# The written order behind the last attention: router, far bounds, expert rounds and scatter in a four-layer image kernel

## The chip, the cores and the metric

One core of one Trainium2 chip runs the whole program. The metric is the device time of one execution in microseconds (us); lower is better. The core has five engines that work at the same time and meet through semaphores: TensorE (PE: matrix products and transposes), VectorE (DVE), ScalarE (ACT), GpSimd (POOL) and SyncE (SP, which here only starts transfers). Each engine works through its own list of instructions in the order written. Transfers run on sixteen DMA engines that all queues share.

## The reference

Four images of 56 x 56 points with 128 channels go through four layers. Layer 0 is attention over 7 x 7 neighbours with a multilayer perceptron; layer 1 a gated recurrence in the Fourier domain; neither is touched. Layers 2 and 3 see an image as 3136 tokens:

```python
t = t + L2_attn(ln(t))     # full softmax attention
t = t + L2_ffn(ln(t))      # 8 experts, the best 2 of each token, softmax weights
t = t + L3_attn(ln(t))     # scores exp(-|q-k|^2), softmax over the scores
t = t + L3_ffn(ln(t))      # expert choice: 64 experts each take their 8 likeliest tokens
```

L3_ffn takes `probs = softmax(logits, over tokens)`; each of the 64 experts picks its 8 largest, pools their tokens by weight, applies two products (128 to 512 to 128) with a gelu between, and adds the result to those 8 tokens, weighted again. In L3_attn the distances are so large that every score is 0 in float32 and the softmax is even: the kernel adds the mean of the values, and proves for the data at hand that this holds, by bounds on all distances (the "far bounds"). If the proof fails, a general program runs afterwards.

## The kernel before, in words

A token tile has P = 112 tokens; a group has GT = 4 tiles (GW = 448 tokens); an image has NG = 7 groups. The four attentions of layer 2 run one after the other on TensorE (`Attention.run`, L2088), and almost everything else of layers 2 and 3 is cut into small pieces and put between their matmuls: `Paced` (L1625) releases pieces from a list in proportion to their written costs, `merged` (L3048) blends lists. Images 0 to 2 are done in this way beside the following attention. Image 3 has no following attention: its mixture and far steps trail the last attention by one group, and what is left is written out by hand in `layers_of_safe_scores` (L2989 to L3044), where the framework keeps the written order on PE, DVE, ACT and POOL. I call this part the tail. Its steps:

- **Last group of the mixture** (`Mixture.parts`, L1479): normalisation (`span_norms`, L1647: variance on DVE, the power -1/2 on POOL at L1662, offset on DVE at L1664), tokens on ACT and POOL (`normal`, L1671), transposes (L207), router product, best two, then for each tile j of four `all_experts` (L1553): two products for eight experts, weighting and a sum of eight. Tiles 0 and 2 are weighted (L1576) and added (L1582) on DVE, tiles 1 and 3 weighted on ACT (L1570) and added on POOL. The weighted tile has two buffers.
- **Far step of the last group**: again normalisation and transposes, then the mean of the values (L1872) is added to x (L1881): groups 0 to 2 on DVE, 3 to 6 on POOL.
- **Router of the expert choice** (`ExpertChoice.steps`, L2271): `statistics` (DVE), `root` for groups 0 to 2 and for 3 to 6 (`inverse_root`, L907: Newton's steps on DVE), `store` (rows of x to DRAM on SP), then for each group `tokens` (xn: two tiles on ACT, two on POOL), `turned` (four transposes on PE, copy to zT on ACT, L2311), `logits` (product L2316 on PE, copy on ACT L2320, eight largest on DVE L2321). xn has two buffers.
- **Choice**: `choose` (DVE search L2340; four indirect gathers issued by POOL, L2344), `marked` (DVE replace L2352, exponential of 3136 columns on ACT L2358, reciprocal L2359, copies L2362), `gather` (DVE products and sums L2372 to L2378), `pooled` (L2383 to L2388), which ends with the experts' input.
- **Far bounds** (`bounds`, L1840): a small product d_ps on PE (L1850), then a maximum on DVE (L1856) or a sum of what exceeds a limit on ACT (L1862). Two bounds make a "half"; image 3 has 91 halves (84 of two, 7 of one). `beside(by, n)` (L2983) places the next n halves; what remains goes into the expert rounds.
- **Expert rounds** (`experts`, L2398): NQ = 16 rounds of ET = 4 experts. `first(q)`: product h_ps from weight lot 2q, copy on ACT. `turned(q)`: four transposes, bias on DVE (L2452), gelu on ACT (L2459). `second(q)`: 32 small products with lot 2q + 1, copy `found` on DVE (L2471), four stores of it to `outs` on SP (L2478). Lots are 1 MB each; nine (UNITS) fit, the first nine are loaded ahead (L2252), each later one when its predecessor in the buffer has been used. A round q does `first(q)`, `turned(q - 1)`, `second(q - 2)`, with paced bounds in three places.
- **Decision and scatter**: `decide` (L1916) closes the proof; `scatter` (L2495) for two pairs of images adds the last found, scales it and adds a bias product, multiplies it with the sparse weights (L2518), adds to x on DVE (L2530) or by an ACT copy and POOL (L2527, L2528), and stores x on SP (L2531).

Of the kernel before, what the change touches and what calls it, by code (L numbers as in the profile page):

```python
# [19 lines left out]
P = 2 * W  # L20
NT = TOK // P
GT = 4
# [1414 lines left out]
class Mixture:  # L1437
# [41 lines left out]
    def parts(self, b, span, places):  # L1479
# [73 lines left out]
        def all_experts(g, j):  # L1553
            gate = held["gate"][:, span.index(g) * GT + j, :]
            gated = sp.tile([P, NE, C], F32, tag="gated", name="gated")
            by_scalar = shared and j % 2
            for i in range(2):
                if by_scalar:
                    pool, tag = (flow.ps_scores, "s") if j == 1 else (flow.ps_sums, "o")
                    y_ps = pool.tile([P, 4, C], F32, tag=tag, name="y_ps")  # L1560
                else:
                    y_ps = flow.one([P, 4, C], "y_ps")
# [3 lines left out]
                )  # L1566
                if by_scalar:
                    for e in range(4):
# [78 lines left out]
def span_norms(env, small, b, span, places, shift=0.0):  # L1647
# [4 lines left out]
    def take():  # L1652
# [4 lines left out]
        out["rs"] = rs = small.tile([P, n], F32, tag=f"g_rs{n}_{places}", name="g_rs")  # L1657
        if n > GT:
            inverse_root(env, small, var, rs)
        else:  # L1660
            nc.vector.tensor_scalar(var, var, 1e-5, None, ALU.add)  # L1661
            nc.gpsimd.tensor_tensor(rs, var, env.exponent[:P, :n], ALU.pow)  # L1662
        out["off"] = off = small.tile([P, n], F32, tag=f"g_off{n}_{places}", name="g_off")
        nc.vector.scalar_tensor_tensor(off, mean2, -0.5, rs, ALU.mult, ALU.mult)  # L1664
        if shift:
# [541 lines left out]
class ExpertChoice:  # L2207
# [46 lines left out]
    def pieces(self, b, places="d"):  # L2254
# [5 lines left out]
        for g in range(NG):  # L2260
# [4 lines left out]
        return first + [  # L2265
            costing(5.0, steps["choose"]), costing(5.0, steps["marked"]),
            *[costing(0.7, lambda g=g: steps["weighed"](g)) for g in range(NG)],
            costing(0.1, steps["gather"]), costing(1.0, steps["pooled"], True),
        ]

    def steps(self, b, places, norms_of):  # L2271
# [78 lines left out]
        def marked():  # L2350
# [7 lines left out]
            nc.scalar.activation(taken, taken, AF.Exp, bias=held["least"], accum_out=total)  # L2358
            nc.vector.reciprocal(inverse, total)  # L2359
            held["inverse"] = both = sp.tile([2 * EC, 1], F32, tag="c_both", name="c_both")  # L2360
# [19 lines left out]
        def pooled():  # L2380
# [12 lines left out]
            statistics=statistics, root=root, store=store, tokens=tokens, turned=turned,  # L2393
            logits=logits, choose=choose, marked=marked, weighed=weighed, gather=gather,
            pooled=pooled,
        )

    def experts(self, ctx, pool, units, others=()):  # L2398
# [13 lines left out]
        for b in range(B):  # L2412
# [4 lines left out]
            )  # L2417
        h, g, used = {}, {}, set()

# [41 lines left out]
        def second(q):  # L2461
# [14 lines left out]
            for b in range(B):  # L2476
                at = b % 2 * EC + ET * q
                nc.sync.dma_start(self.outs[b // 2][at : at + ET], by_image[b])  # L2478

        others = Paced(list(others))  # L2480
        slots = 3 * (NQ + 2)
# [12 lines left out]

    def scatter(self):  # L2495

        env, nc, flow = self.env, self.env.nc, self.flow
        for pair in range(2):
# [3 lines left out]
            nc.vector.tensor_tensor(out, out, o_ps[:, :C], ALU.add)  # L2502
            bias = self.late.tile([2 * EC, C], F32, tag="c_bias", name="c_bias")
            nc.vector.tensor_scalar(bias, self.bias2, self.inverse[pair], None, ALU.mult)
            nc.vector.scalar_tensor_tensor(
                out, out, self.inverse[pair], bias, ALU.mult, ALU.add
            )
            for g in range(NG):
                tiles = slice(g * GT, (g + 1) * GT)
                ys = [  # L2510
# [375 lines left out]
def layers_of_safe_scores(env: Env, f, soft):  # L2886
    with ExitStack() as ctx:
# [100 lines left out]
        with tc.manual_schedule(  # L2988
# [5 lines left out]
            *tail, products, with_norms = held["tails"][-1]  # L2994
            beside("scalar", 5)
            run_all(tail[:6])
            run_all(tail[6:10])
            run_all(tail[10:])
# [7 lines left out]

            def each(name, groups):
                run_all([lambda g=g: of[name](g) for g in groups])

            for g in late:  # L3010
                add[g]()
            for g in early:
# [44 lines left out]
def layers_of_any_scores(env: Env):  # L3057
# [9 lines left out]
    with ExitStack() as ctx:  # L3067
# [22 lines left out]
        choice.experts(ctx, lots, UNITS)  # L3090
        choice.scatter()

# [27 lines left out]
```

## Time and profile before

| What | us |
|---|---|
| Median of 3 runs (lowest, highest) | 2468.28 (2467.14, 2473.53) |
| Profiled execution: its own time | 2469.86 |
| Its span, first to last instruction | 2467.9 |
| Busy in the span: PE / DVE / ACT / POOL | 2337.2 / 1806.8 / 1560.5 / 289.6 |
| Last o_ps matmul of the last attention ends | 2245.25 |
| First l_ps product of the image-3 router | 2291.07 |
| First h_ps product of the expert rounds | 2336.09 |
| First y_ps product of the scatter | 2434.68 |

The page gives busy time of the engines in 40 slices, the granted TensorE clock (PEclk, in tenths) and the bytes moved. The chain of waits goes back from the last instruction to what released it at each step; groups are instructions of one line, operation and tile, with busy time, mean in ns and the idle time before them; the timeline lists instructions with start and length; the table of windows gives busy time by stretch. Most of the program is attention with TensorE at 9 tenths or more in a slice.

### The profile page before, as it was taken

The numbers are of one execution on the slowest core, as the hardware profiler recorded it, in microseconds if no ns is written. First come the engines' busy times: TensorE is split into PE (matmuls) and PEld (weight loads), VectorE is DVE, ScalarE is ACT, GpSimd is POOL, SyncE is SP. The second block draws the span as 40 slices with busy tenths as digits, with TensorE's granted clock in tenths as the row PEclk, the third lists the DMA queues.
The fourth block names the chain that finished last, engine by engine and source line by source line (L and its number), as shares of the span: only waits on it lengthen the run. The fifth ranks groups of instructions, "written<-read, shape, count | busy, mean of one in ns | idle before, by whom it ended". The sixth has DMA issues, their size and how long they took to land.

```text
span 2467.9 us, 38789 instructions
## 1 busy us (share of the span) xinstructions
PE 2337.2 (95%) x14357; PEld 1256.4 (51%) x14357; DVE 1806.8 (73%) x4798; ACT 1560.5 (63%) x3382; POOL 289.6 (12%) x578
## 2 busy tenths in 40 slices
PE   5999999999999999999999999999999998997585
PEld 3777777775555555555554444445444433343134
DVE  5566899983898859699678777854788676775554
ACT  3899889875675646666432556575545566764583
POOL 4323354320000000000000000100000001012202
PEclk9999999999999999999999999999999998998587
DMA  6000000000000000000000010000000010101585
GB/s 143 14 10 2 2 2 2 2 2 9 1 1 1 1 1 0 1 1 1 12 1 0 1 27 1 5 1 1 1 1 1 1 27 5 27 5 53 151 304 177
DMA packets 65642, 61.42 MB, mean 25 GB/s; under 512 B 17048, under 2 KB 60915, under 8 KB 61348
## 3 DMA queue, kind: packets, MB, share of 16 engines
q1 hardware_dynamic: 64932, 57.80, 8.2%
q8 instruction: 115, 1.88, 0.3%
q0 software_dynamic: 512, 1.06, 0.2%
q14 instruction: 83, 0.68, 0.1%
HBM read 45.83 MB, written 12.90 MB: 24 GB/s over the span
## 4 chain that ended last, share of the span: by engine, by line
PE 63%; DVE 6%; ACT 3%; DMA 2%; POOL 1%; issue 1%; SPq 0%; DVEq 0%; ACTq 0%; POOLq 0%
PE s_ps L2055 20%; PE o_ps L2138 20%; PE y_ps L1563 7%; PE d_ps L1850 3%; PE xT_ps L207 2%; PE g_ps L1196 2%; DMA lot<-in_L_ffn_lots 1%; PE l_ps L2316 1%; ACT d_ps L1862 1%; PE y_ps L2079 1%; PE q_ps L1814 1%; PE z_ps L2031 1%; PE l_ps L1523 1%; ACT xn L1682 1%; DVE found L1856 1%
## 5 line engine op out<-in xcount | busy, mean ns | idle before, releaser
L2062 ACT ACTIVATE e<-s_ps 128x448 f32<-128x448 f32 x688 | 366.9, 542 | 501.4 <-PE s_ps L2055 495.9
L2055 PE MATMUL s_ps<-zT,xnT 128*128 128x448 f32 (+1 forms) x1400 | 648.7, 553 | 0.0
L2138 PE MATMUL o_ps<-e,keep 128*128 128x448 f32 (+1 forms) x1376 | 647.3, 553 | 0.0
L2138 PEld LDWEIGHTS o_ps<-e,keep 128*128 128x128 f32 (+1 forms) x1376 | 241.8, 190 | 218.4 <-issue 217.9
L2055 PEld LDWEIGHTS s_ps<-zT,xnT 128*128 128x128 f32 (+1 forms) x1400 | 241.4, 189 | 214.0 <-issue 194.3
L1862 ACT ACTIVATE d_ps<-d_ps,half 128x448 f32<-128x448 f32 (+1 forms) x394 | 238.5, 607 | 80.9 <-PE d_ps L1850 79.8
L1856 DVE TENSOR_REDUCE found<-d_ps 128x1 f32<-128x448 f32 x306 | 185.7, 618 | 86.8 <-PE d_ps L1850 84.8
L1563 PE MATMUL y_ps<-experts,xnT 128*112 128x512 f32 x448 | 216.3, 607 | 0.0
L1576 DVE TENSOR_TENSOR gated<-y_ps,gate 112x512 f32<-112x512 f32 x220 | 148.4, 685 | 34.1 <-PE y_ps L1563 31.8
L1850 PE MATMUL d_ps<-q_near,k_near 32*128 32x448 bf16 (+1 forms) x700 | 138.1, 379 | 20.9 <-ACT d_ps L1862 13.7
L1582 DVE TENSOR_TENSOR gated<-gated 112x512 f32<-112x512 f32 x330 | 150.7, 464 | 3.3
L207 PE MATMUL xT_ps<-ident,xn 112*128 112x112 f32 x672 | 117.3, 282 | 35.2 <-ACT xn L1682 27.1
L207 PEld LDWEIGHTS xT_ps<-ident,xn 112*128 112x128 f32 x672 | 80.3, 147 | 114.2 <-ACT xn L1682 60.0
L1662 POOL TENSOR_TENSOR g_rs<-var,exponent 112x4 f32<-112x4 f32 x17 | 17.9, 1054 | 993.3 <-DVE var L1661 882.3
L1563 PEld LDWEIGHTS y_ps<-experts,xnT 128*112 128x112 f32 x448 | 77.2, 180 | 98.6 <-issue 62.2
L1850 PEld LDWEIGHTS <-k_near 32*128 32x128 bf16 (+1 forms) x700 | 32.2, 92 | 182.1 <-issue 168.9
L675 DVE TENSOR_TENSOR e<-e,band 112x1792 f32<-112x1792 f32 (+3 forms) x56 | 100.0, 1789 | 15.3 <-ACT e L668 15.3
L1682 ACT ACTIVATE xn<-x,g_off,g_rs 112x128 f32<-112x128 f32 x220 | 93.2, 486 | 28.0 <-DVE g_off L1664 13.1
L780 PE MATMUL f_ps<-w_fc,h 128*112 128x128 f32 x896 | 104.8, 274 | 1.9 <-ACT h L771 1.6
L780 PEld LDWEIGHTS f_ps<-w_fc,h 128*112 128x112 f32 x896 | 99.8, 177 | 5.2 <-ACT h L771 4.8
L766 PE MATMUL h_ps<-zT,w_fc 128*128 128x448 f32 x224 | 88.9, 540 | 0.6 <-ACT zT L760 0.6
L668 ACT ACTIVATE e<-s_ps 112x1792 f32<-112x1792 f32 (+3 forms) x56 | 82.7, 1477 | 5.6 <-PE s_ps L659 2.5
(427 smaller groups left out, 3936.9 us busy)
## 6 DMA issues: line engine op xcount, KB each, us to landing
lot<-in_L_ffn_lots SPq DMA_DIRECT2D x32, 1024.0 KB
out_x<-x SPq DMA_DIRECT2D x28, 224.0 KB
x<-in_x SPq DMA_DIRECT2D x3, 1568.0 KB
rows<-x SPq DMA_DIRECT2D x3, 1568.0 KB
x<-in_x SPq DMA_DIRECT2D x7, 224.0 KB
parts<-in_waves SPq DMA_DIRECT2D x8, 173.0 KB
out<-found SPq DMA_DIRECT2D x60, 2.0 KB
rows<-x SPq DMA_DIRECT2D x1, 896.0 KB
```

The source lines that it names most:

```text
L207: self.nc.tensor.transpose(ps[:, j * P : (j + 1) * P], xn[:, j, :], self.ident[:P, :P])
L780: nc.tensor.matmul(f_ps[:, j, :], h[:, k, j * P : (j + 1) * P], w_fc2[:, k, :], start=(k == 0), stop=(k == 3),)
L1563: nc.tensor.matmul(y_ps, held["xnT"][g][:, j * P : (j + 1) * P], self.experts[:, 4 * i : 4 * i + 4, :], start=True, stop=True,)
L1576: nc.vector.tensor_tensor(gated[:, some, :], y_ps, gate[:, some].unsqueeze(2).to_broadcast([P, 4, C]), ALU.mult,)
L1582: by.tensor_tensor(gated[:, :n, :], gated[:, :n, :], gated[:, n : 2 * n, :], ALU.add)
L1682: env.nc.scalar.activation(xn[:, j, :], env.x[b][:, g * GT + j, :], AF.Identity, bias=norm["off"][:, i : i + 1], scale=norm["rs"][:, i : i ...
L1850: nc.tensor.matmul(d, held["k"][part, 128 * c : 128 * c + n], held["q"][g][part, :], start=True, stop=True,)
L1856: nc.vector.tensor_reduce(self.found[:, self.most : self.most + 1], d, AX.X, ALU.max)
L1862: nc.scalar.activation(d, d, AF.Relu, bias=self.half[:n], accum_out=self.found[:n, self.sums : self.sums + 1],)
L2055: nc.tensor.matmul(s_ps[i * n : (i + 1) * n, :GW], self.xnT[:, at : at + n], zT, start=True, stop=True,)
L2062: nc.scalar.activation(e[:n], s_ps[:n, :GW], AF.Exp)
L2138: nc.tensor.matmul(sums[:, :GW], self.keep[:n, k, :], e[:n], start=(k == 0 and g - 1 not in pairs), stop=last,)
```

## The change

Seven edits, most of them in the tail.

1. `span_norms` of one group, and in the tail `root`, compute power and offset on GpSimd (`power_on_gpsimd`); DVE only adds eps and scales the mean.
2. `all_experts` of the last group: tile 1 as before; of tiles 2 and 3 the first four experts are weighted on ACT, the others on DVE, and all are added on DVE.
3. Halves of bounds: 2 instead of 5 ahead of the last group; three behind the late root instead of two at other places of the router; 4 instead of 8 around choice and gather, and all of these on ACT. In the rounds all halves are dealt to DVE and ACT evenly.
4. The router's order: transposes of a group stand in front of the logits of the group before.
5. The reciprocal of the total becomes its own step (`inverted`), behind the far norms.
6. Expert rounds at a distance of one: `first(q)`, `second(q - 1)`, `turned(q)`. The stores of `found` go to GpSimd's queue.
7. Scatter: bias products made on GpSimd in round 1; `decide` stands at the fourth group of the first pair; three instead of five groups of a pair go by ACT and GpSimd.

```diff
+def power_on_gpsimd(env, mean2, var, rs, off, shift=0.0):
+    nc = env.nc
+    p, n = var.shape
+    nc.vector.tensor_scalar(var, var, 1e-5, None, ALU.add)
+    nc.vector.tensor_scalar(mean2, mean2, -0.5, None, ALU.mult)
+    nc.gpsimd.tensor_tensor(rs, var, env.exponent[:p, :n], ALU.pow)
+    nc.gpsimd.tensor_tensor(off, mean2, rs, ALU.mult)
+    if shift:
+        nc.gpsimd.tensor_scalar(off, off, 1.0, shift, ALU.mult, ALU.add)
...
-            by_scalar = shared and j % 2
+            by_scalar = shared and j == 1
...
-                if by_scalar:
+                if by_scalar or shared and j > 1 and i == 0:
...
-            inverse_root(env, sp, var, rs[:, of])
-            nc.vector.scalar_tensor_tensor(off[:, of], mean2, -0.5, rs[:, of], ALU.mult, ALU.mult)
+            if last:
+                power_on_gpsimd(env, mean2, var, rs[:, of], off[:, of])
...
-                nc.sync.dma_start(self.outs[b // 2][at : at + ET], by_image[b])
+                nc.gpsimd.dma_start(self.outs[b // 2][at : at + ET], by_image[b])
...
-        for q in range(NQ + 2):
-            others.step((3 * q + 1) / slots)
+        for q in range(NQ + 1):
             if q < NQ:
                 first(q)
                 more(2 * q)
-            others.step((3 * q + 2) / slots)
-            if 0 < q <= NQ:
-                turned(q - 1)
-            others.step((3 * q + 3) / slots)
-            if q > 1:
-                second(q - 2)
-                more(2 * (q - 2) + 1)
+            others.step((q + 0.3) / NQ)
+            if q == 1:
+                self.biases()
+            if q > 0:
+                second(q - 1)
+                more(2 * (q - 1) + 1)
+            if q < NQ:
+                turned(q)
+            others.step((q + 1) / NQ)
+
+    def biases(self):
+        nc = self.env.nc
+        for pair in range(2):
+            bias = self.bias2 if pair else self.late.tile([2 * EC, C], F32, tag="c_bias", name="c_bias", bufs=1)
+            nc.gpsimd.tensor_scalar(bias, self.bias2, self.inverse[pair], 0.0, ALU.mult, ALU.add)
+            self.bias.append(bias)
...
             for g in range(NG):
+                if (pair, g) == (0, 3):
+                    between()
...
-                    if half and g not in (3, NG - 1):
+                    if half and g in (0, 2, 4):
...
-            beside("scalar", 5)
+            beside("scalar", 2)
...
-            each("statistics", late)
-            beside("scalar", 1)
-            of["tokens"](0), of["tokens"](1), of["turned"](0), of["logits"](0)
+            each("s3 s4 s5 s6 n0")
             of["root"](late)
             of["store"](late)
-            of["turned"](1), of["tokens"](2), of["logits"](1), of["turned"](2), of["logits"](2)
-            beside("scalar", 1)
-            of["tokens"](3), of["tokens"](4), of["turned"](3)
-            of["tokens"](5), of["logits"](3), of["turned"](4)
-            of["tokens"](6), of["logits"](4), of["turned"](5), of["logits"](5)
-            of["turned"](6), of["logits"](6)
-            of["choose"]()
-            beside("scalar", 2)
-            products()
+            for _ in range(3):
+                beside("scalar", 1)
+            each("n1 t0 t1 l0 n2 t2 l1 l2 n3 t3 n4 t4 l3 n5 t5 l4 n6 t6 l5 l6")
+            of["choose"]()
+            products()
             beside("scalar", 1)
             of["marked"]()
             with_norms()
-            beside("both", 6)
+            of["inverted"]()
+            beside("scalar", 1)
+            beside("scalar", 2)
             of["gather"]()
             of["pooled"]()
-            others = [
-                lambda i=i, half=half: half("scalar" if i % 3 == 2 else "both")
-                for i, half in enumerate(halves)
-            ]
+            others = list(halves)
...
-            far.decide()
-            choice.scatter()
+            choice.scatter(far.decide)
```

In `each`, n, t, l and s stand for `tokens`, `turned`, `logits` and `statistics` with the group's number.

More of the change, by code (lines that the diff above doesn't have):

```diff
@@ L1555, in all_experts @@
             gated = sp.tile([P, NE, C], F32, tag="gated", name="gated")
-            by_scalar = shared and j % 2
+            by_scalar = shared and j == 1
             for i in range(2):
-                if by_scalar:
+                if shared and j % 2:
                     pool, tag = (flow.ps_scores, "s") if j == 1 else (flow.ps_sums, "o")
@@ L1566, in all_experts @@
                 )
-                if by_scalar:
+                if by_scalar or shared and j > 1 and i == 0:
                     for e in range(4):
@@ L1657, in take @@
         out["rs"] = rs = small.tile([P, n], F32, tag=f"g_rs{n}_{places}", name="g_rs")
[L1658 to L1662, printed above, removed]
         out["off"] = off = small.tile([P, n], F32, tag=f"g_off{n}_{places}", name="g_off")
+        if n == GT:
+            power_on_gpsimd(env, mean2, var, rs, off, shift)
+            return
+        inverse_root(env, small, var, rs)
         nc.vector.scalar_tensor_tensor(off, mean2, -0.5, rs, ALU.mult, ALU.mult)
@@ L2266, in pieces @@
             costing(5.0, steps["choose"]), costing(5.0, steps["marked"]),
+            costing(0.2, steps["inverted"]),
             *[costing(0.7, lambda g=g: steps["weighed"](g)) for g in range(NG)],
@@ L2294, in root @@
             mean2, var = moments(env, sp, f"c{len(groups)}", st[:, of, :])
-            inverse_root(env, sp, var, rs[:, of])
-            nc.vector.scalar_tensor_tensor(off[:, of], mean2, -0.5, rs[:, of], ALU.mult, ALU.mult)
+            if last:
+                power_on_gpsimd(env, mean2, var, rs[:, of], off[:, of])
+            else:
+                inverse_root(env, sp, var, rs[:, of])
+                nc.vector.scalar_tensor_tensor(
+                    off[:, of], mean2, -0.5, rs[:, of], ALU.mult, ALU.mult
+                )
             if groups[0] == 0:
@@ L2358, in marked, with inverted @@
             nc.scalar.activation(taken, taken, AF.Exp, bias=held["least"], accum_out=total)
-            nc.vector.reciprocal(inverse, total)
+            held["total"] = total
+        def inverted():
+            nc.vector.reciprocal(inverse, held["total"])
             held["inverse"] = both = sp.tile([2 * EC, 1], F32, tag="c_both", name="c_both")
@@ L2393, in steps @@
             statistics=statistics, root=root, store=store, tokens=tokens, turned=turned,
-            logits=logits, choose=choose, marked=marked, weighed=weighed, gather=gather,
-            pooled=pooled,
+            logits=logits, choose=choose, marked=marked, inverted=inverted, weighed=weighed,
+            gather=gather, pooled=pooled,
         )
@@ L2417, in experts @@
             )
-        h, g, used = {}, {}, set()
+        h, g, used, self.bias = {}, {}, set(), []
         def more(u):
@@ L2477, in second @@
                 at = b % 2 * EC + ET * q
-                nc.sync.dma_start(self.outs[b // 2][at : at + ET], by_image[b])
+                nc.gpsimd.dma_start(self.outs[b // 2][at : at + ET], by_image[b])
         others = Paced(list(others))
-        slots = 3 * (NQ + 2)
-        for q in range(NQ + 2):
-            others.step((3 * q + 1) / slots)
+        for q in range(NQ + 1):
             if q < NQ:
@@ L2486, in experts, with scatter @@
                 more(2 * q)
-            others.step((3 * q + 2) / slots)
-            if 0 < q <= NQ:
-                turned(q - 1)
-            others.step((3 * q + 3) / slots)
-            if q > 1:
-                second(q - 2)
-                more(2 * (q - 2) + 1)
-    def scatter(self):
+            others.step((q + 0.3) / NQ)
[13 more added lines that the diff above has]
+            self.bias.append(bias)
+    def scatter(self, between):
         env, nc, flow = self.env, self.env.nc, self.flow
@@ L2502, in scatter @@
             nc.vector.tensor_tensor(out, out, o_ps[:, :C], ALU.add)
-            bias = self.late.tile([2 * EC, C], F32, tag="c_bias", name="c_bias")
-            nc.vector.tensor_scalar(bias, self.bias2, self.inverse[pair], None, ALU.mult)
             nc.vector.scalar_tensor_tensor(
-                out, out, self.inverse[pair], bias, ALU.mult, ALU.add
+                out, out, self.inverse[pair], self.bias[pair], ALU.mult, ALU.add
             )
             for g in range(NG):
+                if (pair, g) == (0, 3):
+                    between()
                 tiles = slice(g * GT, (g + 1) * GT)
@@ L2994, in layers_of_safe_scores @@
             *tail, products, with_norms = held["tails"][-1]
-            beside("scalar", 5)
-            run_all(tail[:6])
-            run_all(tail[6:10])
+            beside("scalar", 2)
+            run_all(tail[:3])
+            run_all(tail[3:10])
             run_all(tail[10:])
@@ L3005, in layers_of_safe_scores, with each @@
             of = choice.steps(B - 1, "dm", [early, late])
-            def each(name, groups):
-                run_all([lambda g=g: of[name](g) for g in groups])
+            def each(steps):
+                for step in steps.split():
+                    of[{"n": "tokens", "t": "turned", "l": "logits", "s": "statistics"}[step[0]]](
+                        int(step[1])
+                    )
             for g in late:
@@ L3090, in layers_of_any_scores @@
         choice.experts(ctx, lots, UNITS)
-        choice.scatter()
+        choice.scatter(lambda: None)
 def tile_kernel(tc, ins, out):
```

## The prediction, made before the changed kernel ran

> **What bounds the kernel now.** I read the page first: busy time in slices.
>
> ```profile
> PE   5999999999999999999999999999999998997585
> PEclk9999999999999999999999999999999998998587
> GB/s 143 14 10 2 2 2 2 2 2 9 1 1 1 1 1 0 1 1 1 12 1 0 1 27 1 5 1 1 1 1 1 1 27 5 27 5 53 151 304 177
> ```
>
> TensorE is full for 90% of the span; the change leaves that part's matmuls alone. The last slices differ: lower clock, gaps, and the only heavy transfers. In the chain of waits the last attention ends with ten o_ps matmuls at 2245.25 us; what follows, the tail, takes 2467.9 - 2245.3 = 222.6 us. I split it by the table of windows (columns: stretch, length, busy time of PE, PEld, DVE, ACT, POOL with counts, granted clock, DMA share, GB/s).
>
> ```profile
> 2289.00:2317.00 28.00, 20.16 (x48) 6.71 (x48) 10.63 (x43) 15.18 (x35) 6.07 (x14) 0.50 0.77 185
> 2345.00:2355.00 10.00, 8.19 (x57) 2.91 (x55) 4.01 (x8) 8.56 (x22) 0.00 (x0) 0.56 0.57 195
> 2355.00:2365.00 10.00, 9.27 (x116) 4.06 (x114) 6.05 (x11) 9.40 (x27) 0.00 (x0) 1.00 0.56 204
> 2375.00:2385.00 10.00, 8.47 (x107) 3.79 (x106) 5.99 (x11) 8.69 (x25) 0.00 (x0) 1.00 0.97 369
> ```
>
> The first row is the router of the expert choice, at half clock with TensorE only 72% busy. The others are the expert rounds: ACT and PE limit them up to about 2365, then the loads of the weight lots (DMA share 0.97, 371 GB/s from 2375 to 2405, so 1.049 MB / 371 = 2.83 us a lot, 5.7 us a round). Between 2345 and 2365 the DMA idles 43% although lots are still due. The waits of the sync queue say why:
>
> ```profile
> SPq L2478 <- DMA lot<-in_L_ffn_lots: 20.1, 14, 2.3
> SPq L2478 <- DVE found L2471: 9.8, 7, 2.2
> ```
>
> The small stores of expert results (L2478, four a round) stand in SP's queue between the lot loads, and wait 20.1 us for earlier lots to land and 9.8 us for their data: the next lot stands behind them.
>
> **Mixture of the last group.** ACT runs ten bounds of 0.61 us ahead of the normalisation (2247.51 to 2253.62), while its offset has been ready since 2251.10. With four bounds ACT is free at 2249.95 and the offset decides: -2.3 us. Dealing: today tile 3 is weighted on ACT only when GpSimd has let go of tile 1's buffer (2267.72) and then added on GpSimd until 2273.19. Dealt anew DVE does it: after tile 2 (half of it now by ACT, 1.1 us) at 2269.2, then 0.65 + 1.48 + 0.29 and four statistics of 0.95, end 2272.65 against 2273.52: -0.9. The far norm's offset moves to GpSimd, a 0.22 us product (row of L904) for two engine changes: +0.2. Sum -3.0. For groups 0 to 5 the same move lies beside attention's matmuls: 0; without that cover 0.2 us a norm.
>
> **Roots on GpSimd, router order.** Price of a power, from the costliest groups on GpSimd:
>
> ```profile
> L901 POOL TENSOR_TENSOR off<-apart_g,exponent 112x4 f32<-112x4 f32 x33 | 33.4, 1012 | 2.5
> L901 POOL TENSOR_TENSOR off<-apart_g,exponent 112x28 f32<-112x28 f32 x3 | 14.4, 4807 | 0.2
> ```
>
> (4.81 - 1.01)/24 = 0.158 us a column: 12 columns 2.3 us, 16 columns 2.9 us. Early root: variance at 2286.37, power to 2288.75, product to 2289.05, against 2288.85 for Newton's fourteen DVE steps: +0.2. DVE goes straight to the late statistics (16 x 0.2 us) and moments, done 2291.0; late power and product to 2294.3, instead of 2297.5. But GpSimd's queue holds group 1's two tiles behind that power (end 2295.25), so its transposes end at 2295.5; ACT has three halves of bounds meanwhile (2290.0 to 2293.7). Then the period. Today's chain for a group:
>
> ```profile
> 2292.82 0.95 PE xT_ps L207 x4
> ...
> 2293.80 0.54 ACT zT L2311
> ...
> 2294.38 1.75 PE l_ps L2316 x2
> 2296.14 0.95 PE xT_ps L207 x4
> ```
>
> 0.95 + 0.6 + 1.75 = 3.3 us; the next tokens are already made. In the new order the transposes no longer wait for the copy, but ACT, in order, holds the tokens of group n behind the logits copy of an earlier group: logits end, copy 0.57, first token tile 0.5, transposes 1.0 = 2.07, then 1.72 of logits, 3.8 a group. From group 1's transposes: seven logits at 1.72 and five such 2.07 = 22.4 us, so logits end at 2317.9, against 2315.35: **+2.55 us**. The late root's two row stores move ahead of three halves of bounds in the text; in SP's queue they stay behind the nine lots, issued by 2302.5 today and some 3 us earlier then, while the gather reads rows after 2321: 0. If their cover (the choice's 3.4 us search) were gone, they would cost their landing, some 2.5 us. Bounds on the +2.55: -3 if GpSimd gives tiles early, +5 if a two-input DVE step waits out a power (the 1.12 us stall of L936 ended with GpSimd's add).
>
> **Choice, gather.** Today six reductions of bounds stand on DVE (2328.84 to 2332.46) ahead of the gather's products, and the reciprocal waits ahead of the norms. Without them the products start when the inverse is copied: choice to inverse stays 13.8 us (c_found 3.4, marks 3.4, exponential 3.0), start 2330.5 in today's clock with the +2.55 in it, against 2332.38. The query and key products of the far bounds, now ahead of two bounds instead of behind four, put 4 ACT steps (1.7 us) beside the search: 0. The gathers land 6.5 us after their first issue (2077.67 to 2084.14 one image earlier), 2330.1: not later. So **-4.4**; the first round starts 3.0 + 1.9 = 4.9 earlier.
>
> **Expert rounds.** From h(0) to the last result 2336.1 to 2431.3 = 95.2 us. Before it 18 halves (two bounds each) are placed, then 12, so 79 instead of 73 come here, all dealt evenly: ACT 79 x 0.61 + 16 x 1.22 = 68 us, DVE 72 x 0.62 + 16 x 0.98 + 4.6 = 65 us; 4.2 a round, which I take as 4.5 (today's full-clock rounds ran at 4.46). Two rounds at half clock take 11 to 13 us, so engines reach h(15) at +71. Transfers: lots 10 and 11 are free after the first second product, +9.5; SP holds lots alone, 21 lots x 2.83 = 59 + 2 landing, +71. I take +74 for both pressing. Behind it second product, transposes, bias, gelu, the last bounds, second product: 7.5 to 9 us (12.5 today, with a round more). Last result at +83: **-12**; between -4 (rounds stay at 5.2) and -17.
>
> The stores: 60 issues go to GpSimd. No plain one is in the trace; the nearest row is its indirect gather:
>
> ```profile
> 2077.67 1.07 POOL L2344 DMA_INDIRECT c_got<-rows,c_at  x1 [0.35 <-POOL c_at L2342]
> 2079.04 0.94 POOL L2344 DMA_INDIRECT c_got<-rows,c_at  x1 [0.30 <-issue]
> 2080.29 0.95 POOL L2344 DMA_INDIRECT c_got<-rows,c_at  x1 [0.30 <-issue]
> ```
>
> 1.25 us apart, so 5.0 a round beside 4.9: nearly full. Nothing else but two biases (0.45 each) stands there. Started at +9.6, 59 x 1.25 + 2.5 lands at +85.8, where the sum wants them at +83.8: +2 to +3. A plain store has four rows, so it may be 0.6 (no wait), or more. The Trainium skill (DMA: Bandwidth & Descriptors, Issuing engines are not separate DMA queues) speaks against the move: starting transfers from several engines saves only the time to initiate them. By that, 60 x 0.5 us of SP, mostly hidden: gain in the rounds about 0. By the row it is the 30 us of waits that hold lots back; the row decides. A second rule (SBUF — State Buffer, Who interferes with whom): DVE in a two-port mode shuts GpSimd out while it writes descriptors. [...] In the trace the gathers at 2321 to 2326 run beside DVE's 3.4 us replace at the same 0.95; the rounds' DVE work reads mostly PSUM. I take 1.25.
>
> **Scatter.** Deciding leaves the path (2431.3 to 2432.9) and so do the bias products: -1.8. The decision now stands in front of group 3 on DVE and PE, 2.2 us, with two stores of 0.85 us queued to cover it: +0.5. Output stores (24.8 us of DMA) stay the bound behind the first tile. With the store wait +2.5: +1.2.
>
> Sum: -3.0 + 2.55 - 4.4 - 12 + 1.2 = -15.7 us. Span 2467.9 to 2452.2; the profiled execution (2469.86) to 2454.2; the median shown is 1.6 lower, 2468.28 to **2452.6**.
>
> **Rivals.** (1) GpSimd's store price becomes the bound. The final sum waits for the last of 60 stores at 12.1 + 59p behind h(0); gain turns to loss where this passes 83.8 + 18.2 = 102, so at p = 1.52 us. At 1.75 it is 115.3: 31.5 us of wait, 2482. Against it: 0.95 and 0.30 in the row, for 128 rows instead of 4. Chance 0.10, slower. (2) Rounds stay bound by engines: TensorE's order at distance one has less slack, 5.2 us a round, half clock for longer; the rounds give 4 instead of 12: 2460.6. For it: ACT 97% busy in 2365 to 2375. 0.17, half of it within 0.3%. (3) The router slips by 5 and not 2.5, and the change does there the reverse of what its order says; with rounds as forecast and a longer store wait 2459: 0.08, a bit under half within 0.3%. (4) Rounds and stores at their good ends, 2443: 0.08. My forecast: 0.57, 2446 to 2460.
>
> 0.3% (7.4 us) is about what a measurement tells from no change. Faster 0.57 + 0.08 + 0.08 + 0.04 = 0.77; same 0.09 + 0.04 = 0.13; slower 0.10. The range reaches from rival 4's low bound to a store price of 1.5: 2441 to 2467.
>
> **What would show it.** ACT's first xn of the last group 1.3 us or more behind four bounds; 2.3 and 2.9 us powers; l_ps with gaps of 1.1 us ahead of transposes and the router some 2.5 us longer; gather products directly behind the inverse; no store rows in SP's queue, DMA share over 0.9 from about 10 us into the rounds to the last lot, and about 83 us of rounds; GpSimd stores about 1.25 us apart, ending near the last result. Wrong if GpSimd's stores are above 1.5 us, if the clock stays half beyond the third round, or if lots still come apart.

## The result, and the profile after

The changed kernel took 2478.68 us (median of 20 runs, 2471.28 to 2487.64) against 2470.48 for the kernel before (20 runs): ratio 1.0034, interval 1.0025 to 1.0043. It is slower by about 8 us where I forecast 16 us faster. The profiled execution is 2477.99 us with a span of 2476.2, against 2469.86 and 2467.9. Further medians of before below come from other chips, so a run is compared by its ratio to the runs of before beside it.

I cut both tails at the starts of the same events: last group of y_ps products of the last attention, first mean of values on DVE, `choose` on DVE, first h_ps, last `found`, first store of x, end.

| Stretch, us | before | after | difference | forecast |
|---|---|---|---|---|
| attention to the first mean (mixture) | 33.27 | 30.26 | -3.0 | -3.0 |
| to `choose` (router) | 37.43 | 38.84 | +1.4 | +2.55 |
| to first h_ps (choice, gather) | 19.46 | 15.09 | -4.4 | -4.4 |
| to last `found` (expert rounds) | 95.18 | 110.63 | **+15.4** | **-12** |
| to first store of x | 6.18 | 4.56 | -1.6 | -1.8, and a store wait of +2.5 |
| to the end | 30.45 | 32.07 | +1.6 | +0.5 |

Attention also ended 1.2 us earlier; the sum is +8.3, the difference of the spans. One stretch decides. The slices of the changed kernel show it as a lower clock at the end:

```profile
PE   6999999999999999999999999999999999996686
PEclk9999999999999999999999999999999999997677
GB/s 143 13 11 2 2 2 2 2 2 9 1 1 1 1 1 0 1 1 1 12 1 1 0 27 1 5 1 1 1 1 1 1 27 5 27 5 138 131 307 108
```

The table of windows of the changed kernel, for two stretches of the rounds and for all of them (columns as before: length, PE, PEld, DVE, ACT, POOL, granted clock, DMA share, GB/s):

```profile
2348.00:2358.00 10.00, 7.25 (x70) 3.02 (x65) 7.05 (x13) 6.99 (x20) 3.88 (x7) 0.80 0.88 331
2368.00:2378.00 10.00, 7.77 (x66) 3.44 (x65) 6.90 (x14) 6.02 (x17) 4.51 (x8) 0.78 0.92 341
2328.94:2439.57 110.63, 92.31 (x855) 41.66 (x855) 60.95 (x111) 69.08 (x191) 33.92 (x60) 0.73 0.63 220
```

and the rounds of the kernel before:

```profile
2336.09:2431.27 95.18, 79.39 (x843) 33.13 (x841) 47.95 (x87) 75.63 (x214) 0.00 (x0) 0.84 0.70 256
```

In the waits of the sync queue (us in total, times, longest) the rows of stores are gone, as forecast; what the lots wait for now is TensorE, whose products free their buffers (32.9 of the 48.0 us lie ahead of the rounds, where the tenth lot waits for the first h_ps):

```profile
SPq L2263 <- PE h_ps L2451: 48.0, 4, 32.9
SPq L2263 <- PE d_ps L1861: 36.0, 8, 4.8
SPq L2263 <- PE o_ps L2485: 20.2, 11, 2.0
```

So the loads are not the bound: their share is 0.63 over all rounds, 0.88 and 0.92 in the two stretches above, and in the rounds TensorE's weight loads for o_ps wait only 2.4 us in all for a lot. DVE and ACT are busy 55% and 62% of the rounds. TensorE runs 12 products more (the bounds moved here), yet it is busy 12.9 us longer and idle 2.5 us longer: it works at a lower clock. One round, from h_ps to h_ps, on the timeline:

```profile
2371.02 1.07 PE L2451 MATMUL h_ps<-lot,pooledT 128*32 128x512 f32 x8
...
2372.46 1.93 PE L2485 MATMUL o_ps<-lot,c_g 128*32 128x128 f32 x32
...
2374.33 1.13 PE L2464 MATMUL hT_ps<-ident,c_h 128*128 128x128 f32 x4
...
2375.39 0.56 PE L1861 MATMUL d_ps<-q_near,k_near 32*128 32x448 bf16 x4
2375.56 0.69 DVE L2472 TENSOR_TENSOR c_g<-hT_ps,bias 128x512 f32<-128x512 f32 x1 [0.81 <-PE hT_ps L2464]
...
2376.29 0.63 ACT L2479 ACTIVATE c_g<-c_g 128x512 f32<-128x512 f32 x1 [2.31 <-DVE c_g L2472]
...
2376.84 0.34 PE L1861 MATMUL d_ps<-q_near,k_near 32*128 32x448 bf16 x1 [0.89 <-DVE found L1867]
...
2378.18 1.07 PE L2451 MATMUL h_ps<-lot,pooledT 128*32 128x512 f32 x8
```

Behind the transposes TensorE does four bounds, which fill the four PSUM buffers, and stops: DVE does the bias first, ACT waits 2.31 us for that bias with the gelu, and only then do both empty buffers. The round takes 7.16 us. Summed over the whole kernel, nearly all of it in the rounds:

```profile
ACT c_g L2479 <- DVE c_g L2472: 35.8, 15, 2.9
PE d_ps L1861 <- DVE found L1867: 19.1, 30, 1.7
```

And h_ps runs at full clock (1.07 us) while o_ps and the transposes run at half: in rounds at full clock, in other runs, they take 1.08 and 0.75. This repeats from round to round; o_ps products of the changed kernel from 2360 to 2400 us (shortest, median, longest in ns):

```profile
L2485 PE MATMUL o_ps<-lot,c_g x180: 400/421/423, 2359.6 to 2400.0; 128*32 128x128 f32 x180
```

The stop sits where TensorE has little to do and the half clock comes where it has most. The granted clock shows why it repeats: it changes in steps of 3.41 us. Four such steps of these rounds (columns as above):

```profile
2369.05:2372.46 3.41, 2.26 (x18) 0.38 (x13) 2.94 (x6) 2.79 (x8) 1.63 (x3) 1.00 0.97 372
2372.46:2375.88 3.42, 3.42 (x41) 2.23 (x41) 1.72 (x4) 1.52 (x5) 0.83 (x2) 0.50 0.87 272
2375.88:2379.29 3.41, 2.33 (x18) 0.52 (x13) 2.60 (x5) 3.00 (x9) 1.43 (x3) 1.00 0.87 343
2379.29:2382.70 3.41, 3.41 (x42) 2.24 (x41) 0.93 (x3) 1.23 (x4) 0.52 (x1) 0.50 0.76 243
```

A full step, with h_ps and the waiting bounds, has TensorE busy for 2.3 of 3.41 us, and a half step follows. The half step, with o_ps and the transposes, has it busy throughout, and a full one follows. From 2348.57 to 2416.84 us the two take turns without exception, and the nine rounds that start from 2350.49 to 2405.41 last 6.83 us on average: two steps. So the rounds keep time with the clock, and the same products meet the half clock in each of them.

The stores on GpSimd, which I feared, are harmless: their group (busy, mean ns | idle before) is

```profile
L2498 POOL DMA_DIRECT2D out<-found x60 | 33.9, 568 | 77.7 <-DVE found L2491 77.7
```

### The profile page after: what moved, and what is told of

It reads as the page before. It is cut to its first block, busy times and chain, and to the rows that moved or that the text cites. A ratio compares the mean times of both kernels' runs of the same rounds, so it can differ in the third digit from the quotient of the medians.

```text
span 2476.2 us, 38786 instructions
## 1 busy us (share of the span) xinstructions
PE 2345.7 (95%) x14357; PEld 1265.2 (51%) x14357; DVE 1812.6 (73%) x4790; ACT 1547.7 (63%) x3342; POOL 331.2 (13%) x663
## 4 chain that ended last, share of the span: by engine, by line
## 5 line engine op out<-in xcount | busy, mean ns | idle before, releaser
L1873 ACT ACTIVATE d_ps<-d_ps,half 128x448 f32<-128x448 f32 (+1 forms) x376 | 226.8, 603 | 82.3 <-PE d_ps L1861 80.1
L1867 DVE TENSOR_REDUCE found<-d_ps 128x1 f32<-128x448 f32 x324 | 195.1, 619 | 79.8 <-PE d_ps L1861 77.6
L1861 PE MATMUL d_ps<-q_near,k_near 32*128 32x448 bf16 (+1 forms) x700 | 133.1, 379 | 37.0 <-DVE found L1867 19.1
L668 ACT ACTIVATE e<-s_ps 112x1792 f32<-112x1792 f32 (+3 forms) x56 | 82.7, 1477 | 7.0 <-PE s_ps L659 4.0
```

Source lines behind the costliest of these rows:

```text
L1861: nc.tensor.matmul(d, held["k"][part, 128 * c : 128 * c + n], held["q"][g][part, :], start=True, stop=True,)
L1867: nc.vector.tensor_reduce(self.found[:, self.most : self.most + 1], d, AX.X, ALU.max)
L1873: nc.scalar.activation(d, d, AF.Relu, bias=self.half[:n], accum_out=self.found[:n, self.sums : self.sums + 1],)
```

## The experiments

"Rounds" is always first h_ps to last `found` in the profiled execution, so it is one execution: the same loop took 83.4, 84.1, 79.4 and 79.4 us in the four kernels that have it with stores on GpSimd and 151 bounds (loop_two, best, two_scatter, two_order). The ratios are of medians. The first theory behind the result: at distance one nothing stands between `second` and the transposes, the gaps lower the clock, the clock lengthens the round. Rivals: the even dealing, the stores on GpSimd, the further bounds.

### Is it the order, the bounds, or the clock?

**loop_two**: the changed kernel with the old loop.

```diff
-            first(q) / bounds / second(q - 1) / turned(q) / bounds
+            bounds / first(q) / bounds / turned(q - 1) / bounds / second(q - 2)
```

> The changed kernel with one part undone: the expert rounds go back to a distance of two with bounds in three places of a round; stores on GpSimd, even dealing, all else as changed. Theory (order): at a distance of one, second product and transposes follow each other without bounds between, then the bounds come in one block; ACT holds its bounds behind the gelu, TensorE fills four PSUM buffers and stops, its clock falls. So here rounds (first h_ps to last found) of 80 to 88 us instead of 110.6, clock near 1.0, median near 2453 us. Rival (load): twelve more bounds and the dealing make DVE the bound; then 105 us or more and about 2475. Rival (transfers): lots come late whatever the order; above 95 us.

Measured: ratio 0.9917 (0.9901 to 0.9934), rounds 83.4 us.

**turn_first**: `turned(q)` ahead of `second(q - 1)`.

> The changed kernel with the order inside a round changed only: first(q), bounds, turned(q), second(q-1), bounds. The 32 second products then lie over DVE's bias and ACT's gelu, so that ACT is free when the bounds come. Theory (order): 88 to 98 us of rounds, median 2458 to 2467. Rival (load): no change from 110.6 us. Rival (distance): what counts is that one round lies between the products, not where: 105 us or more.

Measured: 0.9948 (0.9930 to 0.9965), rounds 90.4 us at a granted clock of 0.91. TensorE is idle for 17.3 us of these rounds, nearly as long as in the changed kernel (18.3), yet the clock stays full from 2352.33 to 2424.01 us. Two steps of it:

```profile
2372.81:2376.22 3.41, 2.65 (x40) 0.92 (x32) 2.92 (x6) 3.02 (x10) 2.06 (x4) 1.00 1.06 411
2386.46:2389.88 3.42, 2.41 (x48) 1.56 (x45) 2.68 (x6) 2.91 (x8) 0.72 (x2) 1.00 1.00 369
```

So the sum of the gaps does not set the clock.

**no_bounds**: `others = []` in the rounds.

> The changed kernel without the far bounds that stand in the rounds (151 of image 3's bounds are not computed, the proof is left incomplete). Theory (order): TensorE never stops for PSUM buffers; the lots set the pace: rounds 74 to 80 us, DMA share above 0.9 throughout, median near 2445. Rival (transfers): above 95 us. Rival (chain: h, copy, transposes, bias, gelu, second is too long for a distance of one): 95 us or more too, but with a low DMA share.

Measured: 0.9873 (0.9852 to 0.9894), rounds 70.4 us at 346 GB/s.

**fill**: three products of `env.ident` with itself in each round, behind the transposes and the first three or four bounds after them.

> The changed kernel with work added: three products of 128x128x128 in float32 a round, never read, where TensorE waits for PSUM buffers (about 0.6 us at full clock, 1.1 at half). Theory (order, with the clock as its amplifier): TensorE has fewer gaps, clock near 1.0, second 1.08 instead of 1.93 us and transposes 0.75 instead of 1.13: rounds of about 5.7 us, 92 to 100 us in all, faster than the change in spite of more work. If the clock doesn't follow the gaps: up to 16 us longer, 110 to 127 us.

Measured: 0.9955 (0.9939 to 0.9972), rounds 92.4 us:

```profile
2333.49:2425.86 92.37, 85.22 (x951) 44.70 (x951) 60.85 (x111) 68.83 (x191) 33.79 (x60) 0.95 0.73 264
```

TensorE has 96 more records than in the changed kernel (855) and is busy 7 us less, at 0.95 instead of 0.73 of the clock. So more work makes the rounds 18 us shorter: the half clock, not the work, is most of the loss. The order matters (loop_two, turn_first), and so do the bounds (no_bounds, which leaves out their work too).

### Stores, order, places: one part at a time

**before_pool_stores**: the kernel before with `nc.gpsimd.dma_start` for the stores of `found`.

> The kernel before with one edit: the four stores of found of a round go to GpSimd's queue instead of SP's. Theory of the prediction: it is SP's store waits (30 us) that hold the weight lots back, so the rounds, 95.2 us from the first h_ps to the last found, shrink to 84 to 86, the stores cost 0.57 us of issue each and nobody waits for them, and the time falls by 9 to 11 us to about 2460. Rival[...]: at most 1 us, the lots then come apart for the compute they wait for (buffers come free late), and the rounds stay at 94 to 95 us.

Measured: 0.9955 (0.9939 to 0.9970), rounds 82.7 us; no row of stores is left in the sync queue's waits.

```profile
2335.35:2418.05 82.70, 74.10 (x843) 32.20 (x841) 47.80 (x87) 75.05 (x214) 33.20 (x60) 0.89 0.76 295
```

This part of the forecast holds: the stores on SP held the lots back, 12.5 us in the rounds (11 by the ratio), and moving them alone is faster.

**loop_two_sp**: loop_two with the stores on SP.

> The changed kernel with the rounds at a distance of two and the stores of found on SP: of the change in the rounds only the even dealing and the biases made in round 1 are left. If the stores on SP are what held the lots, the rounds go from 83.4 us (distance two, stores on GpSimd) back to about 93 to 95 and the time from 2452 to about 2463. If the even dealing brought the shorter rounds, they stay at 83 to 85 and the time at 2452 to 2454.

Measured: 0.9961 (0.9948 to 0.9975), rounds 94.4 us: the same 11 us from the other side.

**before_loop_one**: the kernel before with the new loop only.

> The kernel before with one edit: rounds in the order first(q), bounds, second(q - 1), turned(q), bounds; stores on SP, dealing and biases as before. Theory: the order alone makes the loss, since no bounds lie between second and the transposes, and the next second waits for bias and gelu of its own round: rounds of 6.7 us at three quarters of the clock, 95 to 108 - 118 us, time +13 to +23 (2483 to 2493). Rival: the order is harmless and it is the even dealing together with it that fills the four PSUM buffers: rounds 90 to 97, time within 5 us of before.

Measured: 1.0006 (0.9996 to 1.0017), rounds 94.2 us. My theory fell as stated: the order alone does not make rounds of 110 us. From the sixth `second` on, all but one took 1.08 us here.

**three_places**: the changed kernel with a third place for bounds.

```diff
                 more(2 * (q - 1) + 1)
+            others.step((q + 0.65) / NQ)
             if q < NQ:
                 turned(q)
```

> The changed kernel with a third place for bounds in a round, between second(q - 1) and turned(q), so that three places share the same 151 bounds. Theory: the missing place is the larger half of the loss: ACT and DVE stop for the 3.1 us of second and transposes and the eight or so bounds behind them then meet four PSUM buffers; with it the rounds fall from 110.6 to 88 - 96 us, time 2456 to 2464. Rival: what costs is that a round's second follows its own bias and gelu at once, which a third place does not change: rounds 105 us or more, time above 2473.

Measured: 0.9934 (0.9910 to 0.9957), rounds 82.5 us. With the same work and the same distance, the two waits shown above are 9.6 and 3.7 us instead of 35.8 and 19.1, here from its waits:

```profile
ACT c_g L2479 <- DVE c_g L2472: 9.6, 13, 1.3
...
PE d_ps L1861 <- DVE found L1867: 3.7, 7, 0.7
```

and TensorE's o_ps products stay at full clock:

```profile
L2485 PE MATMUL o_ps<-lot,c_g x348: 272/273/297, 2350.3 to 2399.9; 128*32 128x128 f32 x174
```

**old_deal**: the changed kernel with every third half on ACT alone.

> The changed kernel with the dealing of before in the rounds (every third half with both bounds on ACT) and everything else as changed: distance one, stores on GpSimd. Theory: distance one and the even dealing together make the loss; the bias of a round stands on DVE between the bounds of two places, and with half of all bounds on DVE they hold the four PSUM buffers and the gelu behind the bias; with a third on DVE the rounds fall from 110.6 to 83 - 88 us and the time to 2452 - 2457. Rival: the twelve more bounds and the stores on GpSimd make it together with the order: rounds above 100, time above 2468.

Measured: 1.0086 (1.0064 to 1.0108), rounds 117.5 us. A plain miss: the even dealing helps, by 7 us of rounds.

### What must be added to the order

Distance one alone gave 94.2 us, the change 110.6. The stores, the twelve more bounds and the earlier start were open.

**one_pool**: before_loop_one with the stores on GpSimd.

> The kernel before with two edits: rounds at a distance of one, stores of found on GpSimd (dealing, number of bounds and everything else as before). Theory A: at distance one a round of about 7 us lets TensorE's clock fall and rise in step with the round, so that h_ps runs at full clock (1.06 us) and o_ps and the transposes behind it always at half (1.94 and 1.13); late lots from SP's stores broke that step in the run with distance one alone (94.2 us), and without them the rounds lock: 105 us or more, time above 2477. Theory B: it needs the twelve more bounds that the change leaves for the rounds, or its earlier start; then these rounds take 82 to 88 us and the time is 2456 to 2462.

Measured: 1.0003 (0.9992 to 1.0015).

```profile
2333.59:2427.86 94.27, 77.46 (x843) 34.07 (x843) 47.96 (x88) 74.41 (x212) 33.07 (x60) 0.87 0.71 259
```

**sp_stores**: the changed kernel with the stores on SP.

> The changed kernel with the stores of found back on SP: distance one, even dealing, 151 bounds in the rounds. Theory A: late lots break the lock, rounds 94 to 100 us, time 2460 to 2467, so faster than with the stores on GpSimd. Theory B (bounds in the rounds, or the start, decide): the lock stays, 105 to 115 us, time 2473 to 2484.

Measured: 1.0026 (1.0012 to 1.0041), rounds 107.9 us. At distance one it makes next to no difference where the stores are: 94.2 and 94.3 us, 107.9 and 110.6. Theory A fell. Distance one therefore takes back what the stores gave (82.7 to 94.3 us).

**kick**: fill with `if q < 4` for the fillers.

> The changed kernel with three filler products of 128x128x128 (4 bytes) in TensorE's waits of rounds 0 to 3 alone; with them in all sixteen rounds the rounds took 92.4 us at a granted clock of 0.95. If the half clock keeps itself going (a slow round makes the gaps that make the next one slow), the kick is enough: rounds 90 to 96 us, o_ps at 1.08 us to the end. If the gaps of distance one are there at full clock too and bring the half clock back by themselves, o_ps goes back to 1.94 us within a few rounds behind the last filler, and the rounds take 100 to 108 us.

Measured: 1.0032 (1.0020 to 1.0044), rounds 104.5 us. The o_ps products while the fillers run and after them:

```profile
L2485 PE MATMUL o_ps<-lot,c_g x96: 272/273/297, 2348.0 to 2360.3; 128*32 128x128 f32 x96
...
L2485 PE MATMUL o_ps<-lot,c_g x176: 272/421/423, 2365.8 to 2401.1; 128*32 128x128 f32 x176
```

Two rounds behind the last fillers the half clock is back, so this order brings it back by itself.

**less**: the changed kernel with `others = list(halves)[6:]`, so 139 bounds in the rounds.

> The changed kernel with six halves (twelve bounds) of the 151 left out of the rounds, so 139 as before the change; the proof is then incomplete. Everything else as changed. Theory B1, the number of bounds decides: rounds 92 to 98 us, as in the kernel before with distance one and stores on GpSimd (94.3), time 2460 to 2467. Rival B2, the earlier start or the even dealing decides and the number doesn't: only the work goes, 0.3 us a bound, rounds 105 to 108 us, time above 2471.

Measured: 0.9946 (0.9929 to 0.9964).

```profile
2330.88:2419.69 88.81, 73.61 (x843) 32.67 (x843) 56.80 (x105) 64.71 (x178) 33.86 (x60) 0.89 0.73 274
```

**one_pool_more**: one_pool without `beside("both", 6)` ahead of the gather, so 151 bounds.

> The kernel before with rounds at a distance of one, stores on GpSimd, and the six halves that stand ahead of the gather left to the rounds, so 151 bounds there instead of 139 (94.3 us). Theory B1, the number of bounds decides: rounds 105 to 115 us; the front starts the rounds 2 to 4 us earlier, so the time is 2477 to 2487. Rival B2 (the start or the even dealing): twelve bounds add 0.3 to 0.5 us each, rounds 97 to 101 us, time 2469 to 2474.

Measured: 1.0081 (1.0062 to 1.0099).

```profile
2335.77:2453.09 117.32, 93.66 (x855) 39.29 (x855) 50.00 (x92) 81.02 (x230) 33.13 (x60) 0.73 0.60 208
```

This settles it from both sides: at distance one twelve bounds cost 21.8 us of rounds in the one kernel and 23.0 in the other (22 and 19 by the ratios), 1.6 to 1.9 us each. The earlier start does not do it: less starts its rounds at 2330.88 and is quick, one_pool_more at 2335.77 and is slow. The dealing only lowers it (117.3 to 110.6). At distance two 139 bounds took 82.7 us and 151 took 79.4 to 84.1; the dealing differs there too, but no such loss shows.

**places_half**: the changed kernel with 0.5 for 0.3 in the first place.

> The changed kernel with the paced bounds shared evenly over the two places of a round (at 0.5 instead of 0.3 of a round's share), so that 4.7 bounds stand in each instead of 2.8 and 6.6. Theory: there are four PSUM buffers, and each bound beyond four in one place makes TensorE wait for DVE and ACT; that wait is what lets the clock fall. With 4.7 in each place the wait mostly goes: rounds 86 to 96 us, time 2454 to 2464. Rival: what counts is that second and the transposes stand together with nothing for DVE and ACT between them (a third place there gave 82.5 us); then the even split leaves 103 us or more, above 2470.

Measured: 1.0001 (0.9988 to 1.0015), rounds 101.7 us: 8.9 us better, between the two expectations. More bounds in one place than there are buffers is thus a part. The rest is not separated: three_places puts bounds ahead of the transposes and also brings the largest place down to 3.3 bounds, below the four buffers. That nothing stands between `second` and the transposes cannot be the whole of it, since nothing stands there in turn_first (90.4 us), which keeps 6.6 bounds in the last place; what it changes is that `second` covers bias and gelu ahead of them.

### The other stages, and faster versions

**two_scatter**: loop_two with `far.decide()` ahead of the scatter and `g not in (3, NG - 1)` again.

> Rounds at a distance of two with the stores on GpSimd (2452 us) and, in the scatter, the decision ahead of it and five of seven groups of a pair by ACT and GpSimd, as before the change; only the bias products stay moved. Theory: the decision at the fourth group stops PE and DVE for 2 us just where the output stores start, and more groups on DVE feed them more slowly; last found to end was 38.9 us and goes to 35.5 - 36.5, the time to 2449 - 2450. Rival: the slow drain is TensorE at half clock there, whatever the order: 38 us or more, 2452 or slower.

Measured: 0.9931 (0.9911 to 0.9950), last found to end 38.8 us against 38.9 in loop_two: no gain.

**two_order**: loop_two with `each("t0 l0 t1 n2 l1 t2 l2 ...")` and n1 ahead of the late root.

> Rounds at a distance of two with the stores on GpSimd (2452 us), and the router in the order of before (logits of a group ahead of the transposes of the next), with the tokens of group 1 also ahead of the late root; roots stay on GpSimd. Theory of the prediction: the new order is 3.84 us a group where the old one is 3.3, so from the first value add to the choice 38.8 us become 36.5 to 37.7 and the time falls by 1 to 2 us. Rival: ACT's three bounds and GpSimd's power set the start and ACT's order the period in either case: 38.5 or more, no change.

Measured: 0.9927 (0.9905 to 0.9948); the router took 39.95 us, 1.2 more than with the new order. A miss: putting the old order beside roots on GpSimd is no way back.

**best**: two_scatter with twenty filler products between the marks and the first round.

> Rounds at a distance of two, stores of found on GpSimd, decision and scatter as before the change (this was 2453 us, 79.5 us of rounds with the first three at half clock), and twenty filler products of 128x128x128 in TensorE's waits between the marks and the first round, so that it starts at full clock. Theory: the first three rounds go from 15.4 us to 13 us, the rounds to 76 to 78, the time to 2449 to 2451. Rival: ACT's 69 us and the lots set the rounds from the second on, the fillers delay the experts' input by 1 to 2 us, and nothing is gained: 2453 to 2455.

Measured: 0.9946 (0.9928 to 0.9964), rounds 84.1 us, first h_ps still 1.94 us. The fillers ran too early: TensorE was idle for 2.0 and 2.6 us behind the first seventeen. So loop_two (0.9917, 2452.27 us) has the lowest ratio of the versions with all bounds, with three_places (0.9934, 2453.66 us) and two_order and two_scatter beside it; their intervals overlap.

## Why the prediction was wrong

The step that failed is "Expert rounds": "4.2 a round, which I take as 4.5", and from it -12 us. It added the engines' work, ACT 68 and DVE 65 us, and the lots, and took the largest. These sizes hold (ACT 69.1, DVE 61.0 us measured), but no engine and no transfer bounds the rounds of the changed kernel; they take 6.9 us each. The term that it put at nothing is the half clock behind the second round: TensorE worked at 0.73 of the clock over all rounds, with o_ps at 1.93 instead of 1.08 us in most of them. (The 4.46 us, too, were the short end: full-clock rounds of before start 4.44 to 5.04 us apart.) What stands in the place of the step is a chain of terms, each from a run:

| From | To | Rounds, us | Term | Time, ratio to before |
|---|---|---|---|---|
| before | stores on GpSimd | 95.2 to 82.7 | -12.5 | 0.9955 |
| | distance one (one_pool) | to 94.3 | +11.6 | 1.0003 |
| | twelve bounds more (one_pool_more) | to 117.3 | +23.0 | 1.0081 |
| | even dealing and the rest (after) | to 110.6 | -6.7 | 1.0034 |

The terms hold for this order of the steps: with the stores still on SP, distance one changes nothing (95.2 to 94.2).

- **The store mechanism** was right, in sign and size: -12.5 us by itself. The 0 that the rule on issuing engines would leave is refuted by before_pool_stores: the gain is not the time to start a transfer but that no waiting store stands ahead of a lot in the queue.
- **The stores' price** was put at 1.25 us, from the indirect gather; a plain one of this size takes 0.57 us. Rival 1 was therefore far off, and the store wait of 2.5 us at the end did not come. The longest store kept GpSimd 0.65 us, so no blocking by DVE shows; as the prediction says, the rounds' DVE work reads mostly PSUM, and no run here tries another kind.
- **Moved bounds** were costed as engine time in the rounds (79 for 73 halves). They cost 22 us there, while the two stages they left, mixture and choice, gained 7.4 us together, not all of it from them. This is the mis-costed move: an edit was priced by its busy time where the price is what it does to gaps and clock.
- **Rival 2** named a part of the right mechanism, less slack for TensorE in the order at distance one and the half clock longer, but took the engines for the bound and put 5.2 us a round on it. I used the clock only for the first two rounds. The condition "wrong if the clock stays half beyond the third round" is what happened.
- **Mixture** -3.0 and **choice** -4.4 came as worked out. **Router**: +1.4 for +2.55. The period was right: transposes start at 2304.54 and 2308.38, 3.84 us a group for the 3.8 forecast. Group 1's transposes end 0.3 us earlier than forecast, counted from the first mean, and from there to the last logits it is 21.6 us instead of 22.4, mostly since two logits that follow each other directly take less than twice 1.72: l5 and l6 3.25 us together, l1 and l2, the last of it at full clock, 3.00.
- **Scatter**: decision and bias products off the path gave -1.6 (forecast -1.8). Then +1.6 instead of +0.5: TensorE waits 2.1 us for the decision at the fourth group. two_scatter undoes that and is not shorter, so the decision's place is not shown to be the cause. The clock of the rounds is not either: with the same scatter, last found to end took 33.4 us in fill, 37.1 in three_places and 39.2 in no_bounds (granted clock 0.95, 0.93 and 0.89 in the rounds), against 36.6 in the changed kernel. This stays open.

Of the gaps themselves: TensorE's idle time in the rounds (length less busy) is 18.3 us in the changed kernel and 6.9 in loop_two, with the same products but for three bounds that stand ahead of its first h_ps; its busy time is 92.3 against 76.5. Of the 27.2 us between them, 11.4 are gaps and 15.8 the longer products. The Trainium skill (TensorE: Matmul & The Clock Gate, A second HAM failure mode: psum-queue depth-cycling) describes such a thing: short stops while PSUM buffers are cycled let the gate swing between half and full. The trace agrees in kind: 1.00 and 0.50 by turns for 68 us. Its plain rule in the section on HAM oscillation, no idle gap above some 3.4 us, would have passed this kernel: the longest stop is 0.89 us in the round shown and 1.75 us in all rounds. What fill and kick show is that work put into these waits keeps the clock up, and that it falls again without it. That the sum of the gaps decides is not so (turn_first). How much of a step TensorE is busy comes nearer: in the changed kernel's rounds the full steps that a half one followed had it busy 49 to 77% of their time, in turn_first those that stayed full 69 to 96%. The two ranges overlap, so the threshold stays open, and with it why 8.7 bounds a round let the clock recover and 9.4 do not.

## What to carry to other kernels

Work that is moved as cover into a loop has to be priced by the place it gets: count how many pieces stand there against the buffers they need, and what the in-order engines behind them wait for. When one order of a loop looks tighter on paper, look for the granted clock and for the same product's duration in different rounds; about 1 us of gaps in each round cost more through the clock than through themselves. And try parts alone: the move of sixty small stores was worth 12.5 us, and the new order took nearly all of it back.

## What the hardware showed that I had not expected

- Filler products that compute nothing shortened the rounds from 110.6 to 92.4 us, at a granted clock of 0.95 instead of 0.73; stopped after four rounds, they leave no lasting effect.
- A clock that moves in step with the loop: h_ps at 1.07 us and o_ps at 1.93 us in the same round, round after round, with the clock changing every 3.41 us and rounds of 6.83.
- A plain small store costs GpSimd 0.57 us, 33.9 us for sixty, less than half the 1.25 us between its indirect gathers.
